# Which engine begins the stores of a four-layer graph network: ScalarE in place of SyncE and GpSimd

## The chip, the cores and the metric

The kernel runs on one core of one Trainium2 chip. The metric is the device time of one execution in microseconds (us). One core has five engines, each with its own queue that is worked through in order: TensorE (PE in the profile, its weight loads PEld), VectorE (DVE), ScalarE (ACT), GpSimd (POOL) and SyncE (SP). SP does no arithmetic; it begins DMAs. ACT and POOL can begin DMAs too. All DMAs of the core move their bytes over the same 16 DMA engines.

## The reference

Four layers over a graph of 2048 nodes and a batch of 8, with 128 features: multi-head attention (MHA), graph attention (GAT), MHA, GAT. All use the same adjacency matrix, which has about 16 neighbours in a row. Cut to what matters:

```python
# layers 0 and 2 (MHA, 8 heads of 16)
scores = einsum('bnhd,bmhd->bhnm', h @ Wq, h @ Wk) / 4;  scores[adj == 0] = -inf
x = layer_norm(h + (softmax(scores) @ (h @ Wv)) @ Wo + bo)
x = layer_norm(x + relu(x @ W1 + b1) @ W2 + b2)
# layers 1 and 3 (GAT)
hw = x @ W;  e = leaky_relu(hw @ a_src [:, :, None] + hw @ a_dst [:, None, :]);  e[adj == 0] = -inf
x = layer_norm(softmax(e) @ hw + x)
```

## The kernel before

The kernel is sparse: it never forms a full score matrix. The 2048 nodes are cut into 32 **units** of 64. For each layer `n` a table in HBM, `tables[n]`, holds what a node gives to its neighbours: keys and values of the whole batch for MHA, projected features for GAT. For each unit the rows of the neighbours are fetched from the table by indirect DMAs (`gather`, L1647, begun by POOL) into a buffer `kv`, of which there are six. One-hot matrices `hot` spread a unit's queries to the gathered rows and add the weighted rows back, by matmuls on PE.

- **Setup (`load`, `project`, `block_list`, `unit_list`).** The input is projected into the table of layer 0: PE multiplies, ACT or DVE copies the result into `trows` (L1447, L1449), and `store` (L1566) writes `trows` to the table, 512 KB each, 32 times. At the same time the adjacency matrix is turned into lists of indices and into a matrix `hot` for each unit. ACT copies `hot` into an 8-bit `hot8` (L1283), and L1287 writes it to HBM (`hots`, 120 KB, 32 times), to be used again. The lists of the later units are made while layer 0 already runs, up to about 813 us. `hot8` has two buffers.
- **MHA, per unit (`opened`, `attention`).** `fetch` loads the unit's `x` (L1351, four buffers) and its 8-bit one-hot matrix (L1362), which ACT widens into `hot` (L1369; three buffers). PE spreads the queries (`qe`, L1710), DVE multiplies them with the gathered keys (L1722) and reduces (L1729), ACT takes the exponential (L1739), POOL weighs the values (L1748), and PE adds them up (L1780).
- **After a unit (`after_attention`, `after_graph`).** Projection, layer norm (L1583, L1593, L1616), the feed-forward part (PE L1481 and L1887, ACT L1877), the new `x` (`xnew`, L1626). `keep` (L1339) stores the new `x` for the next layer (256 KB), and `project` makes the unit's rows of the next table, which L1569 stores in two DMAs of 130 or 256 KB. Of `xnew` and `trows` there are two buffers each.
- **GAT, per unit (`graph`).** Gather, scores and exponentials (DVE L1946 and L1953, ACT L1958), one-hot times weights (DVE L1968), sums on PE (L1984). The 8-bit one-hot matrix is not loaded here.

The order of the work on each engine is fixed when the program is built. Every step is an `op` with a cost for each engine that may do it, a key (a due time, the smaller the earlier) and the tiles that it reads and writes. `Plan.order` plays these steps through with the given costs: an engine that is free takes the ready step with the smallest key, and the order that comes out is the order of the instructions in each queue. So a changed cost or key moves other instructions too. In the lines that follow, the first argument is the cost, and `key` is the due time:

```python
self.op({"SP": 0.45}, lambda e: e.dma_start(out=self.xd[u][:, cols], in_=x.tile), key,
        reads=[x], joins=[self.x_at[u]], dma=P * P * 4 * len(self.blocks))
```

All loads (L1351, L1362, the adjacency matrix L1045, the input L1324, weights L946) and nearly all stores stand in SP's one queue. The first 12 stores of `hots` stand in POOL's queue, between the gathers.

Of the kernel before, what the change touches and what calls it, by code (L numbers as in the profile page):

```python
# [9 lines left out]
F32 = mybir.dt.float32  # L10
# [10 lines left out]
P = 128  # L21
# [13 lines left out]
TG = 5  # L35
# [11 lines left out]
LEAD = 60  # L47
# [551 lines left out]
class Plan:  # L599
# [32 lines left out]
    def cell(self, tag, shape, dtype=F32, name=None):  # L632
        pool = self.pools[tag]
        return Cell(tag, lambda: pool.tile(shape, dtype, name=name or tag, tag=tag))
# [133 lines left out]
class Sparse:  # L768
# [395 lines left out]
    def unit_list(self, u, p, block_aux, key):  # L1164
# [12 lines left out]
            reads=[block_aux],  # L1177
# [98 lines left out]
        def indices(e):  # L1276
# [5 lines left out]
        hot8 = cell("hot8", [P, HOT], F8)  # L1282
        op({"ACT": 1.05}, lambda e: e.activation(hot8.tile, hot.tile, AF.Copy, saturate=False), key, reads=[hot], writes=[hot8])  # L1283
        op(

            {"POOL": 0.75} if u < LEAD // TG else {"SP": 0.45},
            lambda e: e.dma_start(out=self.hots[u], in_=hot8.tile),  # L1287
            key,
            reads=[hot8],
            writes=[self.hots_at[u]],  # L1290
            dma=P * HOT,
# [43 lines left out]
    def keep(self, u, x, key):  # L1335
        cols = self.columns
        self.op(
            {"SP": 0.45},
            lambda e: e.dma_start(out=self.xd[u][:, cols], in_=x.tile),  # L1339
            key,  # L1340
            reads=[x],
            joins=[self.x_at[u]],
            dma=P * P * 4 * len(self.blocks),
        )
# [144 lines left out]
    def project(self, n, u, x, key, of=None, shares=()):  # L1489

        of = of or (lambda: x.tile)
        L, hb = self.layers[n], self.HB
        mha = LAYERS[n] is MHA
        width = 2 * P if mha else P + 2
        if self.blocks.start == 0:
            self.trows = self.cell(("trows", "hidden", "trows")[u % 3] if n == 0 else "trows", [P, hb * width], name="trows")
        rows = self.trows
        halves = (0, 1) if self.made is None else (self.blocks.start // 2,)
        kind = "writes" if self.made is None else "joins"
        for v in halves:  # L1500
            at = 2 * v - self.blocks.start
            tag = ("m", "m", "acc", "m", "m", "sums")[(2 * u + v) % 6] if n == 0 else "m"
            ps = self.cell(tag, [P, 2, 256], name="ps_p") if n == 0 else self.bank("ps_p", [P, 2, 256])

            def products(e, ps=ps, at=at):
                for b in range(2):
                    cols = slice((at + b) * P, (at + b + 1) * P)
                    if mha:
                        e.matmul(ps.tile[:, b, :], lhsT=of()[:, cols], rhs=L["Wkv"], start=True, stop=True)
                    else:  # L1510
                        e.matmul(  # L1511
                            ps.tile[:, b, 0 : P + 2], lhsT=of()[:, cols], rhs=L["Wx"], start=True, stop=True
                        )

            self.op({"PE": 1.1 if mha else 0.7}, products, key, reads=[x, self.keys_at if n == 0 else self.weights_at[n]], writes=[ps], holds=[rows], shares=shares)
            if n == 0:
                self.gates[u] = Cell()
                self.gates[u].writers = list(ps.writers)
            if mha:
                self.op(  # L1520
                    {"ACT": 0.6, "DVE": 0.65} if n == 0 else self.either(0.6, 0.68),
                    lambda e, ps=ps, v=v: self.copy(
                        e,
                        rows.tile.rearrange("p (k b d) -> p k b d", k=2, b=hb)[:, :, 2 * v : 2 * v + 2, :],
                        ps.tile.rearrange("p b (k d) -> p k b d", k=2),
                    ),
                    key,
                    reads=[ps],
                    **{kind: [rows]},
                )  # L1530
            else:

                def fill(e, ps=ps, v=v):
                    row = rows.tile.rearrange("p (b d) -> p b d", b=hb)
                    self.copy(e, row[:, 2 * v : 2 * v + 2, 0 : P + 1], ps.tile[:, :, 0 : P + 1])
                    if v:
                        self.copy(e, row[:, :, P + 1], self.ones[:, 0:hb])

                self.op(
                    self.either(0.4 + 0.2 * v, 0.4 + 0.1 * v),  # L1540
                    fill,
                    key,
                    reads=[ps],
                    **{kind: [rows]},
                )

                def spread_out(e, ps=ps, v=v):
                    shape = [P, P // GROUP, 2]
                    e.tensor_tensor(
                        self.t[:, u].rearrange("p (g b) -> p g b", b=hb)[:, :, 2 * v : 2 * v + 2],  # L1550
                        ps.tile[:, :, P + 1].unsqueeze(1).to_broadcast(shape),
                        self.strip[:, :, 0:2],
                        ALU.mult,
                    )

                self.op({"DVE": 0.17}, spread_out, key, reads=[ps], **{kind: [self.t_at[u]]})

        if halves[-1] == 0:
            return

        half = hb * width

        def store(e):
            if n == 0:
                by_half = self.tables[0].rearrange("n (h c) -> (n h) c", h=2)
                e.dma_start(out=by_half[u * P : (u + 1) * P, :], in_=rows.tile)  # L1566
                return
            for part, nodes, hf in self.parts(u):
                e.dma_start(out=self.tables[n][nodes, hf * half : (hf + 1) * half], in_=rows.tile[part])  # L1569

        self.op(
            {"SP": 0.9 if n else 0.45}, store, key, reads=[rows], joins=[self.at(n, u)], dma=P * half * 4
        )

    def norm(self, r, key):

# [628 lines left out]
```

## Time and profile before

| What | Value |
|---|---|
| Time of three runs | 2985.49 us median (2976.74 to 2986.78) |
| The profiled execution | 2981.53 us; its span 2979.8 us |
| Busy share of the span | PE 79%, DVE 77%, POOL 72%, ACT 47% |
| Moved by DMA | 1022.93 MB, mean 343 GB/s |
| DMAs begun by SP that the change touches | L1566 32, L1339 99, L1569 192, L1287 20 |
| DMAs begun by POOL that the change touches | L1287 12 |

The span is the time from the first to the last instruction of the profiled execution; the 1.7 us beside it are start and end. A busy share is an average over stages with different limits. Issuing a DMA does not count as busy time of its engine. A line "A waited for B" gives the idle time of engine A just before an instruction, put down to what ended it.

### The profile page before, as it was taken

What the parts mean: (1) busy time and instruction counts of PE and PEld (TensorE: products, weight loads), DVE (VectorE), ACT (ScalarE), POOL (GpSimd) and SP (SyncE); (2) the same over time, 40 slices, a digit from 0 to 9 for tenths busy, and PEclk for the clock granted to TensorE, in tenths of its full rate; (3) what the DMA queues carried; (4) which work ended last, traced back from release to release, by engine and by line L of the source; (5) the groups of instructions that cost most, each with busy time, mean ns of one, the idle gap of its engine ahead of it and who ended that gap; (6) DMA issues with size and microseconds to landing.
All of it is one profiled execution on the core that took longest, in us unless ns stands there. A gap on an engine that the chain in (4) does not pass through costs nothing. (4 is left out here: it accounts for less than half of the span.)

```text
span 2979.8 us, 60236 instructions
## 1 busy us (share of the span) xinstructions
PE 2346.3 (79%) x22064; PEld 1401.5 (47%) x22064; DVE 2302.5 (77%) x3775; ACT 1414.5 (47%) x4821; POOL 2138.6 (72%) x1459
## 2 busy tenths in 40 slices
PE   7877888888878787687777688888888887777775
PEld 6733444444433334576665243334333333566664
DVE  6779998899887777555554888988898898576665
ACT  4535555455544443455554144444444444354443
POOL 1158887788887875666664778878888786677774
PEclk8759999899999888889998789999999999887887
DMA  7749998888898886999998998999998997899996
GB/s 288 304 180 361 353 348 308 337 321 341 338 352 320 321 306 254 358 408 407 396 404 323 352 350 341 376 347 363 365 369 345 358 365 279 324 406 399 400 398 265
DMA packets 248495, 1022.93 MB, mean 343 GB/s; under 512 B 39232, under 2 KB 53312, under 8 KB 176288
## 3 DMA queue, kind: packets, MB, share of 16 engines
q0 software_dynamic: 166464, 864.44, 74.9%
q1 hardware_dynamic: 81728, 154.55, 14.1%
q8 instruction: 177, 2.90, 0.4%
q14 instruction: 126, 1.03, 0.1%
HBM read 978.59 MB, written 88.08 MB: 358 GB/s over the span
## 5 line engine op out<-in xcount | busy, mean ns | idle before, releaser
L1647 POOL DMA_INDIRECT kv<-table,idx x1152 | 1198.0, 1040 | 588.0 <-issue 285.2
L1748 POOL TENSOR_TENSOR kv<-kv 128x2048 f32<-128x2048 f32 (+1 forms) x259 | 926.6, 3589 | 96.9 <-ACT kv L1739 92.7
L1722 DVE TENSOR_TENSOR kv<-qe,kv 128x2048 f32<-128x2048 f32 (+1 forms) x320 | 662.0, 2069 | 115.0 <-DMA kv<-table,idx 69.9
L1729 DVE TENSOR_REDUCE s<-kv 128x128 f32<-128x2048 f32 (+1 forms) x320 | 659.5, 2061 | 9.3
L1710 PE MATMUL qe<-q_sb,hot 32*128 32x512 f32 (+1 forms) x2304 | 398.2, 695 | 156.0 <-DVE kv L1722 152.3
L1780 PE MATMUL acc<-kv,hot 128*32 128x512 f32 (+1 forms) x2304 | 370.0, 656 | 47.0 <-POOL kv L1748 24.7
L1984 PE MATMUL acc_q<-kv,w 128*32 128x129 f32 (+1 forms) x4608 | 202.1, 308 | 121.5 <-DVE w L1968 96.9
L1968 DVE TENSOR_TENSOR w<-hot,e 128x512 f32<-128x512 f32 (+1 forms) x384 | 221.2, 597 | 50.3 <-ACT e L1958 37.0
L1710 PEld LDWEIGHTS qe<-q_sb,hot 32*128 32x128 f32 (+1 forms) x2304 | 106.7, 196 | 289.5 <-DVE kv L1722 235.2
L1739 ACT ACTIVATE kv<-s 128x128 f32<-128x128 f32 (+1 forms) x320 | 95.3, 298 | 300.2 <-DVE s L1729 193.2
L1984 PEld LDWEIGHTS acc_q<-kv,w 128*32 128x32 f32 (+1 forms) x4608 | 158.2, 126 | 151.5 <-DVE w L1968 109.5
L1946 DVE TENSOR_TENSOR e<-te,kv 128x16 f32<-128x16 f32 (+1 forms) x320 | 58.3, 182 | 215.7 <-DMA kv<-table,idx 212.8
L1583 ACT ACTIVATE junk<-ps_c 128x128 f32<-128x128 f32 x494 | 136.5, 276 | 158.6 <-PE ps_c L1471 140.7
L1447 ACT COPY trows<-ps_p 128x258 f32<-128x258 f32 (+1 forms) x240 | 113.8, 476 | 187.9 <-PE ps_p L1511 103.7
L1780 PEld LDWEIGHTS sums<-kv,hot 128*32 128x32 f32 (+1 forms) x2304 | 90.1, 120 | 212.4 <-issue 206.8
L1958 ACT ACTIVATE e<-e 128x16 f32<-128x16 f32 (+1 forms) x320 | 64.9, 212 | 243.6 <-DVE e L1953 238.3
L1471 PE MATMUL ps_c<-centre,r 128*128 128x128 f32 x1024 | 153.3, 296 | 32.3 <-DVE r L1857 15.6
L1481 PE MATMUL ps_f<-x,W 128*128 128x512 f32 (+1 forms) x264 | 155.7, 674 | 23.5 <-ACT hidden L1877 16.2
L1471 PEld LDWEIGHTS ps_c<-centre,r 128*128 128x128 f32 x1024 | 132.3, 202 | 74.1 <-DVE r L1857 33.7
L1984 PE MATMUL acc<-kv,w 128*32 128x129 f32 (+1 forms) x2304 | 116.4, 303 | 50.1 <-DVE w L1968 36.2
L1887 PE MATMUL ps_y<-hidden,W 128*128 128x512 f32 (+1 forms) x264 | 146.7, 644 | 6.2 <-ACT hidden L1877 5.7
L1780 PEld LDWEIGHTS acc<-kv,hot 128*32 128x32 f32 (+1 forms) x2304 | 55.7, 115 | 197.6 <-issue 107.6
(201 smaller groups left out, 4015.2 us busy)
## 6 DMA issues: line engine op xcount, KB each, us to landing
x<-xd SPq DMA_DIRECT2D x96, 256.0 KB
xd<-xnew SPq DMA_DIRECT2D x93, 256.0 KB
kv<-table,idx POOLq DMA_INDIRECT x1152
table<-trows SPq DMA_DIRECT2D x128, 130.0 KB
kv<-adj_dram SPq DMA_DIRECT2D x16, 1024.0 KB
table<-trows SPq DMA_DIRECT2D x32, 512.0 KB
table<-trows SPq DMA_DIRECT2D x64, 256.0 KB
kv<-xk_dram SPq DMA_DIRECT2D x8, 1024.0 KB
```

The lines of the kernel that those rows point to most:

```text
L1471: e.matmul(ps.tile[:, cols], lhsT=flat(x.tile)[:, cols], rhs=self.centre, start=True, stop=True)
L1481: lambda e: e.matmul(ps.tile, lhsT=w, rhs=x.tile, start=True, stop=True),
L1583: e.activation(self.junk, x, AF.Square, scale=P**-0.5, accum_out=var.tile[:, b, 1:2])
L1647: e.indirect_dma_start(out=rows(kv.tile, j), out_offset=None, in_=self.tables[n][0:nodes], in_offset=bass.IndirectOffsetOnAxis(ap=self.idx ...
L1710: e.matmul(qe.tile[:, j, hf, :], lhsT=hot.tile[rows, t * P : (t + 1) * P], rhs=q.tile[rows, :], start=True, stop=True,)
L1722: e.tensor_tensor(k, qe.tile[:, 0:tiles].rearrange("p j h c -> p (j h) c"), k, ALU.mult)
L1729: e.tensor_reduce(s.tile[:, 0 : tiles * heads].rearrange("p (q c) -> p q c", q=2 * tiles), k, axis=mybir.AxisListType.X, op=ALU.add,)
L1748: e.tensor_tensor(v, v, w.unsqueeze(3).to_broadcast([P, 2 * tiles, heads // 2, HD]), ALU.mult)
L1780: e.matmul(out[rows, :], lhsT=hot.tile[:, col : col + GROUP * (3 - tiles)], rhs=rhs[:, 2 * j + hf, :], start=(t == 0), stop=(t == TG - 1),)
L1887: lambda e, f=f, ps=ps: e.matmul(ps.tile, lhsT=L["W2"][:, f, :], rhs=hidden.tile[:, f, :], start=(f == 0), stop=(f == FFN // P - 1),),
L1968: e.tensor_tensor(w.tile[:, :, j : j + tiles, :].rearrange("p x j c -> p j x c"), oh[:, j : j + tiles].unsqueeze(2).to_broadcast(shape), e ...
L1984: e.matmul(acc(b)[at : at + GROUP * (3 - tiles), :], lhsT=w.tile[:, hf * hb + b, j : j + 3 - tiles, :].rearrange("p j c -> p (j c)"), rhs= ...
```

## The change

Three groups of stores are begun by ACT: the table rows (L1566 and L1569), the new `x` between layers (L1339), and the 8-bit one-hot matrices (L1287), which before were begun by POOL for units 0 to 11 and by SP for the others. Their cost in the plan falls from 0.45 (0.75 on POOL, 0.9 for two table stores) to 0.1 (0.2), and their due time is 3 earlier. The one-hot matrix is described to the DMA as 240 four-byte elements in a partition in place of 960 one-byte ones; the bytes are the same. The stores of the final output stay on SP, the gathers on POOL. Since the plan is played through with new costs, the order of other instructions changes too.

```diff
         op(
-            {"POOL": 0.75} if u < LEAD // TG else {"SP": 0.45},
-            lambda e: e.dma_start(out=self.hots[u], in_=hot8.tile),
-            key,
+            {"ACT": 0.1},
+            lambda e: e.dma_start(out=self.hots[u].bitcast(F32), in_=hot8.tile.bitcast(F32)),
+            key - 3,
             reads=[hot8],
             writes=[self.hots_at[u]],
             dma=P * HOT,
...
     def keep(self, u, x, key):
         cols = self.columns
         self.op(
-            {"SP": 0.45},
+            {"ACT": 0.1},
             lambda e: e.dma_start(out=self.xd[u][:, cols], in_=x.tile),
-            key,
+            key - 3,
...
-        self.op(
-            {"SP": 0.9 if n else 0.45}, store, key, reads=[rows], joins=[self.at(n, u)], dma=P * half * 4
-        )
+        self.op({"ACT": 0.2 if n else 0.1}, store, key - 3, reads=[rows], joins=[self.at(n, u)], dma=P * half * 4)
```

## The prediction

> **What bounds the kernel now.** I read the page first: busy shares, the slices, the chain.
>
> ```profile
> PE 2346.3 (79%) x22064; PEld 1401.5 (47%) x22064; DVE 2302.5 (77%) x3775; ACT 1414.5 (47%) x4821; POOL 2138.6 (72%) x1459
> DMA  7749998888898886999998998999998997899996
> DMA 8%; DVE 7%; PE 6%; issue 4%; POOL 2%; ACT 2%; POOLq 0%; SPq 0%; DVEq 0%; ACTq 0%
> ```
>
> No engine is full; the 16 DMA engines come nearest, at 0.9 in most slices. The chain of waits reaches back only to 2094 us, so its shares add to 30%, not to 100%: 8 points of 30 are gathers landing, 7 DVE, 6 PE, 2 ACT. SP's own queue has 0%: begun stores as such cost nothing. What the change can touch is what waits *behind* a store in SP's or POOL's queue. For that I took the waits, of the core and of SP's queue:
>
> ```profile
> ACT hot L1369 <- DMA hot<-hots: 83.1, 27, 6.2
> POOL hots L1287 <- ACT hot L1283: 124.1, 9, 42.2
> ACT trows L1447 <- DMA table<-trows: 14.5, 5, 5.7
> SPq L1351 <- DVE r L1857: 702.1, 61, 45.7
> SPq L1339 <- ACT xnew L1626: 282.1, 49, 22.9
> ```
>
> ACT stands 83.1 us (27 times) for a one-hot matrix that is late. POOL stands 124.1 us at stores of `hots`. SP stands 282 us at L1339 for a row of `xnew` that ACT has yet to write, with loads behind it. One such place, in SP's timeline of layer 2 (start, us, instruction):
>
> ```profile
> 2331.94 0.33 SPq L1351 DMA_DIRECT2D x<-xd  x1
> 2340.30 0.32 SPq L1339 DMA_DIRECT2D xd<-xnew  x1
> 2340.67 0.42 SPq L1362 DMA_DIRECT2D hot<-hots  x1
> 2343.45 1.09 SPq L1569 DMA_DIRECT2D table<-trows  x2
> ```
>
> SP is free at 2332.3, waits 8 us for `xnew`, and only then begins the load of `hot`. It lands at 2350.33, 9.66 us later, and the chain of waits has this piece ("2340.67 9.66 DMA hot<-hots"): ACT's next steps and PE's feed-forward matmuls come after it.
>
> The second place is the start of layer 0. POOL's timeline (the bracket is the idle time before):
>
> ```profile
> 136.36 0.56 POOL L1287 DMA_DIRECT2D hots<-hot  x1 [0.86 <-ACT ends L1186]
> 153.82 0.62 POOL L1287 DMA_DIRECT2D hots<-hot  x1 [8.25 <-ACT hot L1283]
> 183.32 1.08 POOL L1647 DMA_INDIRECT kv<-table,idx  x1 [6.79 <-PE sums L1780]
> ```
>
> and the table by stage (PE, PEld, DVE, ACT, POOL busy, clock, DMA share, GB/s):
>
> ```profile
> 160.00:183.00 23.00, 15.45 (x78) 6.35 (x78) 18.22 (x16) 9.81 (x23) 8.46 (x4) 0.50 0.19 68
> 183.00:225.00 42.00, 31.98 (x180) 14.29 (x180) 35.67 (x48) 10.79 (x34) 35.25 (x21) 0.63 0.58 211
> ```
>
> The store begun at 136.36 had eight gathers ahead of it in POOL's queue and landed only at about 152.5, where ACT (idle 4.23 us for it) gets its `hot8` buffer back; SP's first load of `hot`, held for the other buffer, starts at 152.31; ACT widens it at 160.08, PE spreads at 161.1, DVE multiplies at 163.30. All six `kv` buffers are full by then, so the DMA engines stand nearly idle from 160 to 183.
>
> **What the Trainium skill says.** (1) "Perfetto Trace Analysis", section DMA Optimizations: giving loads and stores to different issuing engines may help. The 8 us at 2332 agree. (2) "DMA: Bandwidth & Descriptors", section Issuing engines are not separate DMA queues: all DMAs share the 16 DMA engines, so another issuer saves only issue time. Agreed as to bandwidth: I book no faster transfers. (3) Same page, section Queues, rings and completion order: SP and ACT have a ring each, and a DMA engine alternates between rings with work. The 16 us of a 120 KB store behind gathers fits POOL's ring being one line; no trace here shows a store on ACT's ring. (4) Same page, Anatomy of one DMA: about 50 ns of sequencer dispatch. SP's rows show 320 ns for a whole issue, so I take 50 ns only as a lower end.
>
> **The change, part by part.**
>
> *Start of layer 0.* Stores of `hots` 0 to 11 leave POOL (12 x 561 ns = 6.7 us of POOL time, in idle time, so worth nothing). What counts is the landing: 16 us behind gathers. Begun by ACT after its 8-bit copy and on another ring, I estimate 6 us (the 7.8 us that the first `hot` load took among the gathers, a little shorter). So the first `hot` is widened some 10 us sooner. In the built program ACT's first widening still stands after about ten unit lists, so not all of the 23 us hole can close: gain **10 us**, between 0 (the lists, finished near 148, set it) and 20.
>
> *Layers 0 and 2.* With no stores on SP, L1362 follows L1351 directly; at 2332 that is 8 us sooner. Of the 83.1 us, about 9 belong to the start and the last units; 74 remain (52.7 between 1700 and 2450, 21.3 between 300 and 1090). How much of it is on the path? In the stretch that the chain covers (2094 to 2530) ACT stood 30.8 us for `hot`, ten times, and the chain has 9.66 us of it: 31%. So 0.31 x 74 = **23 us** gained; ends 10% (7 us) and 60% (44 us). What is late next: `qe` waiting for DVE and gathers landing, in the waits of both layers.
>
> *Layers 1 and 3, and the change of layers.* No `hot` is loaded; x loads come four buffers ahead. At the change of layers the table stores were begun at once (trows ready 2528.9, L1569 at 2528.94; 2572.4 and 2572.47), so nothing is gained there. Setup: the 14.5 us of ACT waiting for table stores lie beside a PE that is 85% busy from 50 to 100 us; worth nothing to 5 us, taken as 0.
>
> *What ACT now has to do.* 32 x 0.320 (L1566) + 99 x 0.325 (L1339) + 192 x 0.516 (L1569) + 32 x 0.325 (L1287) = 10.2 + 32.2 + 99.1 + 10.4 = **152 us** of ACT's queue, at SP's prices; ACT would be taken for 53% in place of 47%. At 50 ns an issue it is 355 x 0.05 = 18 us. Behind each stand ACT's exponentials (L1739), on which POOL's L1748 waits (92.7 us now), and norms. ACT's share of the chain is 2% of the span, 60 us, and ACT is busy about 47% of the chain's 886 us, 416 us: 14% of ACT's work is on the path. So 152 x 0.14 = 21 us lost, at the lower end 2.5; a store often waits only for ACT's own last write and may overlap work in flight. I take **10 us**.
>
> *Added waits.* In the built program the DMAs of SP and ACT take turns on eight completion semaphores, so a store on ACT can wait for a DMA eight places earlier, a load among them. With five or six such DMAs per unit and 27.5 us per unit (a period of four units is 110 us in the chain), eight places are some 35 us against landings under 16 us: 0, and if loads are late, a few us inside the upper end. The new order of the plan is worth 10 us either way.
>
> Sum: -10 - 23 + 10 = -23 us. The profiled execution took 2981.53 us (span 2979.8), 4 us under the median of 2985.49; 23 us off the median give **2962 us**.
>
> **Rivals.** *A, slower: the issue time on ACT is on the path.* A table store pair holds ACT 1.03 us (2 x 0.516), right after `trows`, with the next exponential behind it; POOL (72% busy) and the freeing of `kv` follow. Against: ACT is idle half the time, and the plan lets the store fall where ACT is free. It decides once more than 33/152 = 22% of the issue time is on the path (33 is the gain above). At 45%: 68 - 33 = 35 us slower, 3020 us.
> *B, no change: the loads are hidden anyway.* DMA share is 0.94 in layer 2 and DVE is busy 371 of 400 us from 300 to 700; `hot` sooner only makes ACT wait for PE and DVE. For it: of ten waits for `hot` one is on the chain. Then the 23 shrink to 7, the start gives 5, ACT costs 10: 2983 us.
> *C, the change doesn't do what it says:* the stores' place in ACT's queue is fixed by the plan, and a store whose data DVE writes holds ACT as it held SP. Only some 15 copies of `trows` are DVE's, so this is small.
>
> **How the numbers follow.** The gain: 0.66. B: 0.14. A, with C: 0.20. About 0.3% (9 us) is what can be told from no change. B and the weak end of the gain give "same" 0.13, A gives "slower" 0.21, the rest is faster. Strong ends together: 20 + 44 - 2.5 = 61 us, 2924 us, and 12 more for the new order: 2912. Weak ends: 0 + 7 - 21 = 14 us slower, 2999 us. A's far end is left out.
>
> **What would show it.** Right: no stores in SP's list of DMA issues; L1369's wait for `hot` under 25 us; the hole in DMA share at 160 to 183 shorter by 10 us and the first L1722 near 153; ACT issues of 0.3 to 0.5 us. Wrong: L1369 still waiting 80 us (x buffers, not stores, hold SP); L1739 or L1748 waiting some 50 us more with ACT queue pieces in the chain (A); waits gone and the span the same (B).

## The result and the profile after

The changed kernel takes **3005.96 us** (median of five; 2997.78 to 3012.64) against 2985.49 us: the ratio is 1.0077, 95% interval 1.0053 to 1.0101. It is slower by 0.8% where the prediction had it faster by 0.8%; the forecast is 44 us too low, and the time lies above its weak end of 2999 us. The profiled execution took 3012.64 us; its span is 3010.8 us, 31.0 us more than the span before.

From line 1571 on, line numbers are two lower in the changed kernel (L1722 is now L1720, L1968 is L1966, L1748 is L1746, L1780 is L1778). First its page, the same three lines as before: busy shares, DMA share by slice, chain.

```profile
PE 2379.3 (79%) x22064; PEld 1425.6 (47%) x22064; DVE 2301.5 (76%) x3773; ACT 1424.1 (47%) x4823; POOL 2135.3 (71%) x1447
...
DMA  8467898878989886899999798999999998899997
...
PE 15%; DMA 14%; DVE 10%; issue 7%; POOL 5%; ACT 2%; ACTq 0%; POOLq 0%; DVEq 0%
```

The work is the same, and no engine is fuller. The second slice of DMA (75 to 150 us) has fallen from 0.7 to 0.4. Part of the fall is gathers that have moved out of it (the first is begun at 149.1, before the change at 124.7), part is loads that now run in the first slice. The table stores of setup show that time is lost there all the same. Their row, before and after (ns of one issue: min/median/max; start of the first and of the last):

```profile
L1566 SPq DMA_DIRECT2D table<-trows x32: 319/320/528, 13.5 to 127.4; - x32
L1566 ACTq DMA_DIRECT2D table<-trows x32: 326/326/350, 13.6 to 149.3; - x32
```

The last one is begun 21.9 us later. Next a wait of the core, and then those of SP's queue (us in total, times, longest):

```profile
ACT hot L1369 <- DMA hot<-hots: 18.0, 4, 7.3
```

```profile
SPq L1351 <- DVE r L1855: 1563.6, 61, 64.8
...
SPq L946 <- DMA table<-trows: 13.3, 3, 5.9
...
SPq L1324 <- DMA table<-trows: 12.7, 3, 8.3
```

ACT's wait for `hot` has shrunk as forecast (83.1 us before, 18.0 now), and SP waits at L1351 for a free `x` buffer, no longer for the data of a store. But it now waits for table stores to land, at L946 and L1324, of which more below. In SP's timeline of layer 2 the load of `hot` now follows that of `x` at once, where L1339 had stood 8 us between them:

```profile
2340.94 0.32 SPq L1351 DMA_DIRECT2D x<-xd  x1
2341.37 0.38 SPq L1362 DMA_DIRECT2D hot<-hots  x1
```

So this part of the forecast came. To see where the time went, I cut both spans at the first L1722 (end of setup), the first L1968 (layer 1), the first L1722 of layer 2, and the first and last L1968 of layer 3:

| us | setup | layer 0 | layer 1 | layer 2 | layer 3 |
|---|---|---|---|---|---|
| before | 163.3 | 1005.2 | 473.8 | 902.5 | 412.7 |
| changed | 181.0 | 1033.8 | 481.0 | 879.8 | 413.1 |
| difference | +17.7 | +28.6 | +7.2 | -22.7 | +0.4 |

Layer 2 gave 22.7 us; setup and layers 0 and 1 took 53.5. In setup, these rows of ACT's timeline of the changed kernel show one place:

```profile
87.94 0.84 ACT L1207 ACTIVATE hot<-hot,ends 128x640 f32<-128x640 f32 x1
94.58 0.33 ACTq L1566 DMA_DIRECT2D table<-trows  x1
94.94 0.16 ACT L1125 COPY aux<-ps_off 128x4 f32<-128x4 f32 x1 [6.17 <-DMA x<-xt_dram]
```

A store of `trows`, whose data were ready, is held until an unrelated load of an `x` row has landed; ACT is idle 6.17 us, and behind it PE waits 5.05 us for ACT's L1127. The same goes the other way in the two last lines of SP's waits: all of it lies in the first 150 us, where SP waits 13.3 + 12.7 = 26 us for table stores to land before it begins loads of weights and of input, which do not read the table. Before the change it was 2.2 us. The two queues wait for each other: in the built program their DMAs take turns on the same completion semaphores (counters of what has landed), so a DMA can be held until the one that used its counter last has landed.

In layer 0, from 200 to 700 us, while the unit lists are made, DVE is the fullest engine and so the likely bound: it was busy 463.0 of 500 us before (PE 413.2), and 433.3 after. The waits of DVE in that stretch, first of the kernel before:

```profile
DVE t L1549 <- ACT trows L1447: 5.0, 6, 1.5
...
DVE rc L1838 <- PE sums L1780: 1.1, 2, 0.6
```

and of the changed kernel:

```profile
DVE t L1549 <- ACT trows L1447: 22.0, 12, 7.3
DVE rc L1836 <- PE sums L1778: 10.5, 9, 2.6
```

DVE's next instruction in its order now more often needs something that ACT or PE has yet to do. It can be the work of ACT's stores, or of the order itself, since the new costs and keys made every queue's order anew. The experiments separate the two.

### The profile page after: what moved, and what is told of

Same layout as the page of the kernel before. It is cut to its first block, busy times and chain, and to the rows that moved or that the text cites. A ratio compares the mean times of both kernels' runs of the same rounds, so it can differ in the third digit from the quotient of the medians.

```text
span 3010.8 us, 60146 instructions
## 1 busy us (share of the span) xinstructions
PE 2379.3 (79%) x22064; PEld 1425.6 (47%) x22064; DVE 2301.5 (76%) x3773; ACT 1424.1 (47%) x4823; POOL 2135.3 (71%) x1447
## 4 chain that ended last, share of the span: by engine, by line
PE 15%; DMA 14%; DVE 10%; issue 7%; POOL 5%; ACT 2%; ACTq 0%; POOLq 0%; DVEq 0%
DMA kv<-table,idx 14%; DVE kv L1720 4%; POOL kv L1645 3%; PE qe L1708 3%; POOL kv L1746 2%; PE acc L1778 2%; DVE s L1727 2%; PE ps_c L1471 1%; DVE kv L1746 1%; PE ps_y L1885 1%; PE ps_f L1481 1%; PE acc_q L1982 1%; PE ps_q L1799 1%; PE ps_t L1458 1%; PE ps_te L2005 1%
## 5 line engine op out<-in xcount | busy, mean ns | idle before, releaser
L1746 POOL TENSOR_TENSOR kv<-kv 128x2048 f32<-128x2048 f32 (+1 forms) x259 | 924.7, 3582 | 125.3 <-ACT kv L1737 121.4
L1720 DVE TENSOR_TENSOR kv<-qe,kv 128x2048 f32<-128x2048 f32 (+1 forms) x320 | 662.5, 2070 | 117.2 <-DMA kv<-table,idx 66.9
L1778 PE MATMUL acc<-kv,hot 128*32 128x512 f32 (+1 forms) x2304 | 369.4, 650 | 74.5 <-POOL kv L1746 53.8
L1966 DVE TENSOR_TENSOR w<-hot,e 128x512 f32<-128x512 f32 (+1 forms) x384 | 220.6, 597 | 50.5 <-ACT e L1956 38.2
L1447 ACT COPY trows<-ps_p 128x512 f32<-128x512 f32 (+1 forms) x242 | 115.5, 478 | 215.2 <-PE ps_p L1511 111.1
L1778 PEld LDWEIGHTS sums<-kv,hot 128*32 128x32 f32 (+1 forms) x2304 | 90.2, 119 | 210.8 <-issue 204.0
L1471 PE MATMUL ps_c<-centre,r 128*128 128x128 f32 x1024 | 152.3, 295 | 25.2 <-DVE r L1855 13.3
L1458 PE MATMUL ps_t<-ident,normed 128*128 128x128 f32 x638 | 124.6, 314 | 47.5 <-ACT normed L1614 20.5
L1778 PEld LDWEIGHTS acc<-kv,hot 128*32 128x32 f32 (+1 forms) x2304 | 55.7, 115 | 222.0 <-POOL kv L1746 106.1
L1614 ACT ACTIVATE normed<-ps_c,rstd 128x128 f32<-128x128 f32 x494 | 144.6, 370 | 22.2 <-DMA W<-L_W_dram 8.9
```

The lines of the kernel that those rows point to most:

```text
L1458: e.transpose(ps.tile[:, b * P : (b + 1) * P], flat(x.tile)[:, b * P : (b + 1) * P], self.ident)
L1471: e.matmul(ps.tile[:, cols], lhsT=flat(x.tile)[:, cols], rhs=self.centre, start=True, stop=True)
L1614: e.activation(out, in_, AF.Copy, scale=by)
L1720: e.tensor_tensor(k, qe.tile[:, 0:tiles].rearrange("p j h c -> p (j h) c"), k, ALU.mult)
L1746: e.tensor_tensor(v, v, w.unsqueeze(3).to_broadcast([P, 2 * tiles, heads // 2, HD]), ALU.mult)
L1778: e.matmul(out[rows, :], lhsT=hot.tile[:, col : col + GROUP * (3 - tiles)], rhs=rhs[:, 2 * j + hf, :], start=(t == 0), stop=(t == TG - 1),)
```

## The experiments

Two theories stand against each other. **Issuer**: who begins a store decides, by what it holds up. **Order**: the plan, run with other costs, gives another order, and that one is worse. An order can be kept while the issuer changes, since a step's function may call another engine's `dma_start` than the plan's.

Each ratio is to the kernel before on the same chip. The third group ran on a chip where every version took 8% longer (before: 3225 us; layer 1 takes 566 to 587 us there), so of that group only ratios and layer 0 are held against the others. Executions of one kernel spread by some 12 us either way and the stage lengths are from one execution each, so stage differences under 10 us say little by themselves. Stages are held against the profile before that is shown above; the kernel before took 2975 to 2978 us on the chips of the first, second and fourth group, in place of 2985.

### First group: issuer against order

**A, old order, all stores begun by ACT**, the plan's costs and keys left alone:

```diff
-            lambda e: e.dma_start(out=self.hots[u], in_=hot8.tile),
+            lambda e: self.nc.scalar.dma_start(out=self.hots[u].bitcast(F32), in_=hot8.tile.bitcast(F32)),
...
-            lambda e: e.dma_start(out=self.xd[u][:, cols], in_=x.tile),
+            lambda e: self.nc.scalar.dma_start(out=self.xd[u][:, cols], in_=x.tile),
...
         def store(e):
+            e = self.nc.scalar
```

> The kernel before with its plan (order, costs, keys) untouched, and all four stores (table rows of setup and of layers 1 to 3, x rows, one-hot matrices) begun by ACT at the place where the plan had put them for SP or POOL. Theory 'issuer' (a store in ACT's in-order queue waits for a DMA landing or a completion semaphore and holds ACT's copies of trows, so PE stops): the last table store of setup is begun near 149 us as in the changed kernel (before: 127), the first L1722 near 181, the whole some 15 to 25 us slower than before, or worse, since the plan left no room for the stores on ACT. Theory 'order' (the loss comes from the new costs and keys reshuffling the plan): last table store near 127 and first L1722 near 160; with L1369's waits for hot gone the whole is 10 to 25 us faster than before.

Ratio 0.9997 (0.9981 to 1.0013): no difference. Neither theory's numbers came: the last table store is begun at 138.0 us, setup ends at 172.2 (+8.9), layer 0 takes 1007.3 (+2.1), layer 2 takes 880.7 (-21.8). Moving the stores alone leaves layer 0 as it was. A loss in setup and a gain in layer 2 stand against each other; by the stages 12.5 us of gain are left over, of which the medians show nothing (this profile is 5.7 us under its median).

**B, new order, every store begun as before** (an edit of the changed kernel):

```diff
-            lambda e: e.dma_start(out=self.hots[u].bitcast(F32), in_=hot8.tile.bitcast(F32)),
+            lambda e: (self.nc.gpsimd if u < LEAD // TG else self.nc.sync).dma_start(out=self.hots[u].bitcast(F32), in_=hot8.tile.bitcast(F32)),
...
-            lambda e: e.dma_start(out=self.xd[u][:, cols], in_=x.tile),
+            lambda e: self.nc.sync.dma_start(out=self.xd[u][:, cols], in_=x.tile),
...
         def store(e):
+            e = self.nc.sync
```

> The changed kernel's order of instructions kept (its costs and keys plan the stores as ACT's), but each store begun by the engine that began it before: table rows and x rows by SP, one-hot matrices by POOL for units below 12 and by SP after. Theory 'issuer': setup as before, last table store near 127 us, first L1722 near 163; L1369's waits for hot are back at 80 us or so; the whole within 10 us of before. Theory 'order': the last table store stays near 149 us, and with SP blocked again the whole is 20 us or more above the changed kernel, some 3025 us.

Ratio 1.0100 (1.0074 to 1.0126): slower, with no store on ACT at all. Setup ends at 168.9, the last table store is begun at 131.2; layer 0 takes 1024.3 (+19.1), layer 2 900.1 (-2.4). The order accounts for the loss in layer 0, and a few us of that in setup; it brings none of the gain in layer 2. Of the two waits of DVE shown above, 13.2 and 9.3 us are there already. (The stores stand in SP's and POOL's queues where the plan had put them for ACT, so a part of the 1.0% can be theirs; I and J below have no such part.)

**C, the changed kernel with setup's table stores back on SP**, the plan made anew:

```diff
-        self.op({"ACT": 0.2 if n else 0.1}, store, key - 3, reads=[rows], joins=[self.at(n, u)], dma=P * half * 4)
+        self.op({"ACT": 0.2} if n else {"SP": 0.45}, store, key - 3 if n else key, reads=[rows], joins=[self.at(n, u)], dma=P * half * 4)
```

> The changed kernel with the 32 table stores of setup (L1566) back on SP at cost 0.45 and the old key; the plan is made anew; x rows, table rows of layers 1 to 3 and one-hot matrices stay on ACT. Theory 'issuer': the setup's loss of 22 us goes (last table store near 127 to 132 us) and the unblocked loads of the later layers stay: 2965 to 2985 us. Theory 'order' or 'one-hot stores' (the loss is not the table stores of setup): last table store still near 145 to 150, whole 2995 to 3010 us.

**D, the same with the changed kernel's order kept:**

```diff
             if n == 0:
+                e = self.nc.sync
                 by_half = self.tables[0].rearrange("n (h c) -> (n h) c", h=2)
```

> The changed kernel in its own order, with only the 32 table stores of setup (L1566) begun by SP in place of ACT. Theory 'issuer': last table store near 127 to 132 us, ACT's waits for table stores below 15 us, the first L1722 near 163, the whole about 20 us below the changed kernel, 2980 to 2990 us. Theory 'order': within 5 us of the changed kernel, last table store near 149.

C: 1.0043 (1.0030 to 1.0057); D: 1.0044 (1.0031 to 1.0058). Setup ends at 165.2 and 159.7 us: in D, 21.3 us before the changed kernel, with the order the same. Layer 0 stays long (1035.0 and 1029.1), layer 2 short (878.8 and 877.7). So in this order most of setup's loss belongs to who begins the table stores, and layer 0's does not.

### Second group: which part of the issuer's effect

**E, old order, only setup's 32 table stores on ACT** (from here on edits of the kernel before, where nothing else is said):

```diff
             if n == 0:
+                e = self.nc.scalar
                 by_half = self.tables[0].rearrange("n (h c) -> (n h) c", h=2)
```

> The kernel before in its own order, with only the 32 table stores of setup (L1566) begun by ACT. Theory 'shared completions' (a store on ACT waits for the landing of the DMA that last used its completion semaphore, an SP load begun late; seen in the ACT-issued version of the old order as 5.24 us behind the load of bo at 43 to 48 us and 5.88 us behind an x row at 83 to 89): ACT shows waits for landings of SP's loads again, the last table store 5 to 10 us after 127.4, the whole 5 to 10 us slower than before (2980 to 2985). Theory 'issue time' (0.33 us each in ACT's queue, 10 us in all): no such waits, ACT idle as before, and at most 3 us slower.

Ratio 1.0021 (1.0007 to 1.0036). ACT's timeline of E:

```profile
41.79 0.90 ACT L1205 ACTIVATE hot<-slot,ends 128x640 f32<-128x640 f32 x1
47.16 0.36 ACTq L1567 DMA_DIRECT2D table<-trows  x1
47.94 0.59 ACT L1447 COPY trows<-ps_p 128x512 f32<-128x512 f32 x1 [5.25 <-DMA bo<-L_bo_dram]
```

and SP's:

```profile
41.49 0.38 SPq L946 DMA_DIRECT2D b<-L_b_dram  x1
45.69 0.34 SPq L946 DMA_DIRECT2D bo<-L_bo_dram  x1
```

SP begins the 0.5 KB load of `bo` only at 45.69, since it has itself waited 3.8 us for a table store to land; ACT's next store waits for it, ACT with the store, and PE behind ACT. The last table store is begun at 134.5, 7.1 us late. A store takes 0.33 us of ACT's queue; "issue time" does not explain a single wait of 5 us. In A the same wait stands at 47.40 (5.24 us), and one of 5.88 us at 88.61, for a load of an `x` row.

**F, the version with setup kept**: old order; `x` rows, table rows of layers 1 to 3 and `hots` of units 12 to 31 on ACT, the rest as before:

```diff
-            lambda e: e.dma_start(out=self.hots[u], in_=hot8.tile),
+            lambda e: (self.nc.gpsimd if u < LEAD // TG else self.nc.scalar).dma_start(out=self.hots[u].bitcast(F32), in_=hot8.tile.bitcast(F32)),
...
-            lambda e: e.dma_start(out=self.xd[u][:, cols], in_=x.tile),
+            lambda e: self.nc.scalar.dma_start(out=self.xd[u][:, cols], in_=x.tile),
...
         def store(e):
+            e = self.nc.scalar if n else self.nc.sync
```

> The kernel before in its own order: x rows, table rows of layers 1 to 3 and one-hot matrices of units 12 and up begun by ACT; table rows of setup stay on SP, one-hot matrices of units 0 to 11 on POOL. If the gain in layers 1 and 2 (22 us in the profile of the version with all four stores on ACT in this order) and the loss in setup (10 us) are separate sums: last table store near 127 us, first L1723 near 163, L1369's waits under 25 us, the whole 15 to 25 us faster than before, 2950 to 2960. If the gain came only because setup was late, or lies in noise: within 8 us of before.

Ratio **0.9965** (0.9950 to 0.9979): faster than both kernels. Setup ends at 165.0, layer 2 takes 882.9 (-19.6). The size is less than expected, 12 us by the medians and not 15 to 25: layer 0 took 11 us more in the profile, which is itself 13 us over its median. Against A (0.9997), which differs by the stores of setup and of `hots` 0 to 11, it is 0.3% faster, and the intervals do not touch.

**G, the changed kernel with measured costs in the plan** (0.33 for 0.1 at L1287 and L1339 too):

```diff
-        self.op({"ACT": 0.2 if n else 0.1}, store, key - 3, reads=[rows], joins=[self.at(n, u)], dma=P * half * 4)
+        self.op({"ACT": 1.0 if n else 0.33}, store, key - 3, reads=[rows], joins=[self.at(n, u)], dma=P * half * 4)
```

> The changed kernel with the plan's costs for ACT's stores set to what the trace measures (0.33 us in place of 0.1 for one store, 1.0 in place of 0.2 for a pair); engines and keys as in the changed kernel, so only the order differs. Theory 'order' (any new order that the plan makes is some 20 to 25 us worse in layer 0, or this one is worse because costs were understated): layer 0 recovers, one-hot stores end near 820 us in place of 860, while setup stays some 10 us late; the whole 2970 to 2985. Theory 'issuer' (ACT's load is what costs): within 8 us of the changed kernel, some 2995 to 3005 on this chip.

Ratio 1.0122 (1.0096 to 1.0147): a miss for both theories. Layer 0 is as long as with the other new orders (1028.3), so understated costs are not what made it long; and in layer 2 (907.3) even the gain is lost: DVE waits 46.1 us there for gathers to land, where it waited 18.0 before. Its setup ends at 166.6 and the last table store is begun at 133.9, though ACT begins all 32: what these stores cost on ACT hangs on the order too. Truer costs did not make a better order.

**H, as F, with setup's table stores on POOL:**

```diff
-            e = self.nc.scalar if n else self.nc.sync
+            e = self.nc.scalar if n else self.nc.gpsimd
```

> As the version with setup kept, but the 32 table stores of setup begun by POOL in place of SP (before's order; POOL is 9% busy before 100 us). Theory 'shared completions': POOL's DMAs complete on other semaphores than SP's and ACT's, so neither ACT nor SP is held; last table store at 120 to 128 us, the whole 0 to 8 us faster than the version with setup kept. Rival: POOL needs longer for a store than SP and its own setup work waits for trows; last table store 130 us or later, no gain over it.

Ratio 0.9970 (0.9957 to 0.9984), no better than F. The rival held: the last table store was begun at 139.4, since POOL's queue is in order too, and a table store there takes 0.53 us and stands behind stores of `hots` that wait for ACT, and later behind gathers. Setup ends at 173.1, 8.1 us after F's, and the whole is not longer by anything that shows: a later end of setup is not time lost one for one.

### Third group: is it any new order, and which stores give the gain

**I and J, one cost changed by 0.01, no store moved.** I:

```diff
-        op({"ACT": 1.05}, lambda e: e.activation(hot8.tile, hot.tile, AF.Copy, saturate=False), key, reads=[hot], writes=[hot8])
+        op({"ACT": 1.06}, lambda e: e.activation(hot8.tile, hot.tile, AF.Copy, saturate=False), key, reads=[hot], writes=[hot8])
```

> The kernel before with one number of the plan changed and nothing moved: ACT's cost of the 8-bit copy (L1283) is 1.06 in place of 1.05, so every store stays where it was and only the order made from the costs differs. Theory 'tuned order' (any new order loses in layer 0 what the old constants had been fitted for): setup within 5 us of before, the stretch from the first L1722 to the first L1968 20 to 30 us longer than its 1005 us, the whole 15 to 30 us slower than before. Theory 'these stores' (it is the plan's reaction to stores on ACT that makes layer 0 worse): within 8 us of before.

J:

```diff
-        op({"DVE": 1.2}, ones, key + 0.4, reads=[pick, ps_l], writes=[rank, hot])
+        op({"DVE": 1.21}, ones, key + 0.4, reads=[pick, ps_l], writes=[rank, hot])
```

> A second draw of the same kind: the kernel before with DVE's cost of one step of the unit lists (ones) 1.21 in place of 1.2, nothing moved. Theory 'tuned order': as there, 15 to 30 us slower than before, in layer 0. Theory 'these stores': within 8 us of before.

I: 1.0099 (1.0063 to 1.0136), layer 0 1033.8 us. J: 1.0064 (1.0037 to 1.0092), layer 0 1015.6 us, in an execution 15 us under its median. A hundredth of a microsecond in the plan costs about as much as the whole change did. This is the strongest evidence on the order: each of the five other orders tried (the changed kernel's, C's, G's, I's, J's) made its kernel slower than before, whatever the edit meant. Layer 0 takes 1003 to 1020 us in all versions of the old order but one (P below), and 1024 to 1035 us in the others but J. Which moves in layer 0 do it was not singled out, and J's loss cannot be placed in layer 0: on the same chip K and L, in the old order, take 1013.0 and 1019.7 us there.

**K, old order, only the `x` rows on ACT:**

```diff
-            lambda e: e.dma_start(out=self.xd[u][:, cols], in_=x.tile),
+            lambda e: self.nc.scalar.dma_start(out=self.xd[u][:, cols], in_=x.tile),
```

> The kernel before in its own order, with only the x rows between layers (L1339, 99 stores) begun by ACT. SP waited some 340 us at L1339 and 245 us at L1569 in layers 1 and 2. Theory 'SP freed': half of the gain of 22 us in layers 1 and 2 if each kind of wait holds the loads by itself, 8 to 15 us faster than before; if the waits at L1569 now catch the same loads, under 5 us; L1369's wait for hot between 25 and 70 us. ACT's issues cost little either way (32 us of its queue).

**L, old order, only the table rows of layers 1 to 3 on ACT:**

```diff
         def store(e):
+            e = self.nc.scalar if n else e
```

> The kernel before in its own order, with only the table rows of layers 1 to 3 (L1569, 192 stores) begun by ACT. Theory 'SP freed': 3 to 12 us faster than before, the rest of the gain that the x rows leave. Theory 'ACT's issue time' (99 us of ACT's queue on the path at 14 to 45%): 10 to 40 us slower, with ACT's exponentials (L1739) later and POOL's L1748 waiting longer.

K: 0.9939 (0.9915 to 0.9963). L: 1.0005 (0.9986 to 1.0024). The `x` rows alone give more than the half that was expected of them; the table rows alone show neither gain nor cost. Layer 2 took 893.8 us in K, against 912.3, 919.9 and 930.7 in I, J and L on the same chip.

### Fourth group: what to add to the x rows, and the shared completions

**M is K again, N is K with L's edit, O is K with F's edit of `hots`**, on one chip.

> The kernel before in its own order with only the x rows between layers begun by ACT, run again so that it stands beside the two that add to it on one chip. 0.6% faster than before (0.992 to 0.996), with L1369's wait for hot near 37 us; at or under 0.3% would mean that the earlier ratio belonged to the slower chip.

> As that, with the table rows of layers 1 to 3 (L1569) on ACT too; one-hot matrices and setup as before. Theory 'SP freed': SP is then held only by its buffers, L1369's wait falls from 37 to under 20 us, and the whole is 2 to 8 us faster than with the x rows alone. Theory 'ACT's issue time' (192 issues of 0.5 us in front of ACT's exponentials and norms): the loads come earlier but the whole is 5 to 10 us slower than with the x rows alone, POOL's L1748 and the exponentials L1739 waiting longer.

> As the version with x rows on ACT, with the one-hot matrices of units 12 to 31 on ACT too (L1287, stored in layer 0 between 215 and 825 us); table rows stay on SP. Theory: 20 stores of 0.33 us in layer 0 where DVE is the bound; the whole within 5 us of x rows alone, the stretch from the first L1722 to the first L1968 within 8 us. Rival: ACT's stores of one-hot matrices are what made layer 0 longer by 11 us in the version with setup kept; then 5 to 12 us slower than x rows alone.

M: **0.9948** (0.9925 to 0.9972), 2960.85 us against 2978.41. N: 0.9956 (0.9940 to 0.9971). O: 0.9954 (0.9936 to 0.9971). The three cannot be told apart. In N L1369's wait fell from M's 47.7 to 12.4 us, and ACT's queue got 192 issues of 0.484 us, 93 us in all. Neither a gain nor a cost shows: N's median is 6.5 us over M's, inside the intervals. A small gain and a small cost that cancel are not ruled out. SP's timeline of M in layer 2, with table stores still in SP's queue:

```profile
2327.89 0.33 SPq L1351 DMA_DIRECT2D x<-xd  x1
2328.34 0.65 SPq L1362 DMA_DIRECT2D hot<-hots  x1
2339.40 1.24 SPq L1569 DMA_DIRECT2D table<-trows  x2
```

The load of `hot` stands right behind that of `x`; a table store that waits comes after it, and holds only the next unit's loads.

What this buys can be followed in the traces. One place of layer 2 in the kernel before, 110 us ahead of the place that the prediction shows:

```profile
2240.56 0.99 ACT L1369 CAST hot<-hot 128x960 f32<-128x960 fp8e5 x1 [5.49 <-DMA hot<-hots]
2241.46 0.68 ACT L1877 ACTIVATE hidden<-ps_f,b 128x512 f32<-128x512 f32 x1
2242.19 2.07 PE L1481 MATMUL ps_f<-x,W 128*128 128x512 f32 x2 [4.00 <-ACT hidden L1877]
2245.74 0.75 DVE L1857 SCALAR_TENSOR_TENSOR r<-ps_o,bo,x 128x512 f32<-128x512 f32 x1 [4.81 <-PE ps_o L1481]
```

SP began this load of `hot` at 2230.57, after 8 us at a store of an `x` row. ACT stands at L1369 with the finished work of PE behind it (`hidden`, and the copy `at` for the next projection); PE waits for ACT, and DVE, the fullest engine, for PE's `ps_o`. The waits of layer 2 before (1643 to 2545 us) and in M (1645 to 2533 us):

```profile
ACT hot L1369 <- DMA hot<-hots: 57.8, 19, 6.2
DVE r L1857 <- PE ps_o L1481: 21.9, 9, 4.8
```

```profile
ACT hot L1369 <- DMA hot<-hots: 28.5, 11, 4.6
DVE r L1857 <- PE ps_o L1481: 3.9, 4, 1.2
```

This wait of DVE is 3.9 to 4.7 us in layer 2 of each of the eleven versions with the `x` rows on ACT (G too), and 18.6 to 26.8 us in each of the seven others. The half of ACT's wait for `hot` that M keeps no longer reaches DVE this way, which fits that N, almost without it, gains nothing more.

**P, as E, with the weight loads but the first (L946) begun by POOL**, whose completions are counted apart:

```diff
-                    e.dma_start(out=t, in_=a)
+                    (e if at else self.nc.gpsimd).dma_start(out=t, in_=a)
```

> As the version with only setup's table stores on ACT (before's order; last table store 134.5 us, ACT held 5.2 us until the load of bo had landed), with the weight loads of all layers but the first matrices of layer 0 (L946) begun by POOL, whose completions are counted apart. Theory 'shared completions': no wait of ACT for bo or another weight load, the last table store at 127 to 131 us, the whole 3 to 8 us under that version, within 0.1% of before. If another late load on SP takes its place, the wait shows again behind kv<-adj_dram or x<-xt_dram and the store stays at 133 us or later. Theory 'issue time': no change, 134 us.

In setup just what "shared completions" said: no wait for `bo`, and the last table store is back at 127.1. This is the row of the table store's own line (min/median/max ns, first and last start) in E:

```profile
L1567 ACTq DMA_DIRECT2D table<-trows x32: 325/326/365, 13.6 to 134.5; - x32
```

and in P:

```profile
L1567 ACTq DMA_DIRECT2D table<-trows x32: 326/327/344, 13.6 to 127.1; - x32
```

The whole missed: 1.0038 (1.0021 to 1.0056), not within 0.1% of before. Layer 0 took 1026.5 and layer 2 911.6 in a profile that is 13 us over its median. Moving the weight loads deals out the completions of all later DMAs anew too; whether that is the reason was not tried.

## Why the prediction was wrong

**Layers 0 and 2, gain 23: the mechanism right, the place and the term half right.** Layer 2 became 22.7 us shorter in the profile, 19 to 25 us shorter in A, C, D, F, H, N and O, and 13 us in M, all of which have the `x` rows on ACT (G, in yet another order, is the exception); the 16 us that the sum put there, 0.31 of 52.7, are near. That they are is in part luck: the 31% hold the 9.66 us of a load's flight against idle times of ACT, and at that place ACT stood 5.18 us, 17% of the 30.8. Layer 0's share, 0.31 of 21.3 or 6.6 us, is not to be seen (A +2.1, O 0.0 us), though it is too small for single executions to rule out. And the price of a late `hot` is not ACT's wait but what reaches DVE through PE: M keeps 47.7 of 83.1 us of ACT's wait, and N and O, which add to it, are no faster. The Trainium skill, "Perfetto Trace Analysis", section DMA Optimizations, says that it may make sense to give inputs to one issuing engine and outputs to another; for the `x` rows the runs agree (0.5%), for all stores together they show no gain (A: 0.0%).

**Start of layer 0, gain 10, and "setup 0", "added waits 0": the first step that failed.** The stores of `hots` did leave POOL, but the first L1722 came at 181.0, not near 153. I had looked at ACT's 14.5 us wait for table stores, and taken it as covered by a PE that is 85% busy. That wait is 14.5 us after the change too. What I priced at nothing was the new wait: I reckoned with six DMAs per unit and 35 us for eight places, which are layer 0's and 2's numbers. In setup DMAs are begun far closer together, SP's loads start late because they wait for buffers (three loads of the adjacency matrix between 51.74 and 80.42 in the changed kernel) and for ACT's table stores to land (26 us), and behind each table store stand the copies that PE needs to go on. Two such stalls, of 5.2 us at a table store and of 5.9 us at a store of `hots`, are about as much as A's last table store is late, 10.6 us; one of 5.2 us is most of E's 7.1.

**"The new order is worth 10 us either way": the second step that failed, and the larger.** B measures it: 1.0% of the kernel, 30 us. A symmetric guess was the error: the old order was not one order among many, and a cost changed by 0.01 loses 0.6 to 1.0%. What makes the old order better stays open.

**What ACT has to do, loss 10: too dear.** The durations were right (326 ns for L1566 and L1339; 490 ns for L1569, forecast 516). But N against M shows no cost of 93 us of it, nor does L against the kernel before. No store on ACT took less than 0.32 us; the lower end of 50 ns, point (4) of the prediction's list, is stated there for DMAs that GpSimd begins. Rival A had the right sign for another reason: at 22% the 93 us would be 20 us, 0.7% of the time, and no such cost shows in N. Rival C, that a store in ACT's queue holds ACT as it held SP, was called small; it is what happened in setup, though for another DMA's landing and not for the store's own data. Rival B's thought, that earlier loads of `hot` gain nothing, holds for what M had left of them; the other waits did reach DVE, for 18 us in layer 2 (21.9 before, 3.9 in M).

By ratios to before, on whichever chip each was measured: the order +1.0%, all issuers in the new order -0.2% (1.0077 against 1.0100, with intervals that overlap), of which setup's table stores are +0.3% (the changed kernel against D) and the rest -0.6% (D against B). That the one-hot matrix is described in four-byte elements is not told apart from its issuer; O against M shows nothing of either for 20 of the 32, and I and J lose without it.

## What to carry to other kernels

A DMA moved to an engine that computes puts a foreign wait into that engine's queue: ask which completion counter it takes, which earlier DMA used that counter last, and when that one can start. Move the few stores that wait long for their data and have loads behind them (here the 99 of `x` rows, 0.5% faster), and leave those whose new queue feeds the bound. Where a planner makes the order, change issuer and plan apart, and price a new order by a run with a cost changed by next to nothing.

## What was not expected of the hardware

Where a program hands the same completion counters round between two issuing engines, a store whose data are ready can stand in ACT's queue until the other engine's load lands: 6.17 us for an `x` row, 5.25 us for a load of 0.5 KB, with a store's issue itself at 0.33 us. The Trainium skill, "DMA: Bandwidth & Descriptors", section Issuing engines are not separate DMA queues, says that another issuing engine saves only the sequencer's time. Here that time was not what counted on either side: 93 us of it in ACT's queue left no trace (N against M), while the place of a wait in a queue moved layer 2 by 13 to 23 us (M, and the changed kernel).
